# Seven block products in another order, with each bank read by one engine per product

## The chip, the cores and the metric

The kernel runs on one core of one Trainium2 chip. The time is device microseconds of one execution; three executions of the kernel before give a median of 2688.93 us (2687.47 to 2691.13). Five engines work side by side, each with its own queue of instructions: TensorE (PE, with its weight loads as PEld), VectorE (DVE), ScalarE (ACT), GpSimd (POOL) and SyncE (SP). TensorE writes its products to PSUM, which this kernel divides into eight banks of 128 x 512 fp32 each; VectorE and ScalarE read them from there into SBUF.

## The reference: what is computed

The input x has 16 samples of 256 channels and 32 x 32 places. Each sample goes through four layers, all in fp32:

- L0: group norm, q, k and v by 1x1 convolutions, softmax(q·k / 16) over the 1024 places, the weighted sum of v, an output projection, and x added.
- L1: mean and maximum over the channels, two 3x3 convolutions with one output channel, a sigmoid, and the sample multiplied by it.
- L2: like L0 with its own weights.
- L3: q and k of 32 channels, clipped logits, a softmax, the weighted sum of v times gamma, and x added.

```python
xn = group_norm(x, gamma, beta)
attn = jax.nn.softmax(jnp.einsum('bnc,bcm->bnm', q, k) / math.sqrt(C), axis=-1)
out = jnp.einsum('bnm,bmc->bnc', attn, v)                        # L0, L2
energy = jnp.clip(jnp.einsum('bqn,bqm->bnm', q, k) * scale, -10.0, 10.0)
out = jnp.einsum('bcm,bnm->bcn', v, jax.nn.softmax(energy, -1))  # L3
```

## The kernel before

**Two lanes.** Samples 0, 2, 4, ... run in lane 0 and 1, 3, 5, ... in lane 1. Each lane is a Python generator, `stream(0)` and `stream(1)`; they are stepped in turn, the second 30 steps behind the first, so that one sample's matmuls fill the other's waits. A scheduler then sets the final order of each engine's instructions and puts in the semaphores. The last sample's L3 has code of its own, `ending()`, which the change leaves alone.

**Attention.** The weights of L0 and L2 are folded first, so `attend` (L952) needs one product t = m·x in place of q and k, then the values v, then for each half of the queries `logits` (t·x into e, exponentials in place) and `weighted` (e·v). In L3 q and k are computed directly (L1109), the scores s at L1135, their exponentials at L1151 and the clipping at L1160; the values and `weighted` are the same.

**Seven products for eight.** Each of these large products is split into 2 x 2 blocks and computed with seven block products by a scheme of Strassen and Winograd: factors s1 to s4 and t1 to t4 are sums of blocks of the left and right factor, made by VectorE (for the weighted sum at L722, L723, L768 and L773), and partial products are summed in PSUM. Of the four result blocks, (0,0) is 11·11 + 12·21; the others are sums in which the running bank b holds first 11·11, then adds s2·t2, then adds s3·t3, and the bank c holds s1·t1 and then adds s4·22. In the code a product is written `go(left, right, bank)` and ends in `product` (L570), whose matmul is L577, the line that all of them show in the profile. With `fresh=False` it adds to what the bank holds.

**`seven` (L615)** is this scheme for the transform t (banks `tb`, `ta`, `tc`, `tf`), the values (`vb`, `va`, `vc`, `vf`) and the logits (`sb`, `sa`, `sc`, `sf`). `copy(i, j, ps)` is ScalarE's first write of result block (i, j), at L969 for t, L947 for v, L696 for the logits; `plus(i, j, ps)` is VectorE's addition of a bank to a block in SBUF, at L627. In the logits each pair of block rows is followed by its exponentials on ScalarE (L706, L708) as soon as the row is whole.

**`weighted` (L711)** writes the scheme out with three banks: b and c as above, and one bank `af` of which the halves hold 12·21 (`af[:, 0]`) and 22·(-t4) (`af[:, 1]`). Its result is acc in SBUF, of 128 x 4 x 256. Copies by ScalarE stand at L765, L778, L781 and L790, VectorE's additions at L749. v has a column of ones behind its 256, so the bank c gets the sums of the exponentials as a 129th column; their reciprocals are taken from c at L777 and L784, and `done` (L754) multiplies acc by them and adds it to the residual.

**Banks.** Every product takes its bank from one pool of eight, `ps_m`, by `bank()`. A bank is taken again in turn, once its last reader is through. Two engines that touch the same bank are put in order by a semaphore, also where both only read it.

Of the kernel before, what the change touches and what calls it, by code (L numbers as in the profile page):

```python
# [10 lines left out]
FP = mybir.dt.float32  # L11
# [5 lines left out]
P = 128  # L17
C = 256
# [5 lines left out]
TPH = HALF // P  # L24
# [4 lines left out]
STRIP = 32  # L29
# [178 lines left out]
def fast_path(nc, tc, k, bad, x, w_l0, w_l2, w_l3, qk_bias, v_bias, tap_idx, out):  # L208
# [7 lines left out]
    with ExitStack() as ctx:  # L216
# [5 lines left out]
        combp = ctx.enter_context(tc.tile_pool(name="combp", bufs=2))  # L222
# [10 lines left out]
        def bank(nm):  # L233
            return ps_m.tile([P, HALF], FP, tag="m", name=nm)
# [335 lines left out]
        def product(terms, fresh=True, lone=True):  # L570

            first = None
            for i, (out, pairs) in enumerate(terms):
                for m, (left, right) in enumerate(pairs):
                    mm = nc.tensor.matmul(  # L577
                        out,
                        left,
                        right,  # L580
                        start=fresh and m == 0 and (lone or i == 0),
                        stop=(m == len(pairs) - 1),
                        skip_group_check=True,
                    )
                    if first is None:
                        first = mm
                    elif m == 0 and not lone:
                        tc.add_manual_dep(
                            mm.ins,
                            first.ins.name,  # L590
                            mybir.DependencyInfo(
                                mybir.DependencyClass.NoSync, mybir.DependencyReason.DATA
                            ),
                            reason="the first product clears the bank's flags",
                        )
# [19 lines left out]
        def seven(go, copy, block, banks, left, right):  # L615

            b, a, c, f = banks

            def plus(i, j, ps):
                dst = block(i, j)
                if len(dst.shape) == 4:
                    src = ps.rearrange("p (a b n) -> p a b n", a=dst.shape[1], b=dst.shape[2])
                else:
                    src = ps.rearrange("p (m n) -> p m n", m=dst.shape[1])
                nc.vector.tensor_tensor(dst, src, dst, ALU.add)  # L627

            go(left("11"), right("11"), b, lone=False)
            copy(0, 0, b)  # L630
            go(left("12"), right("21"), a)
            plus(0, 0, a)
            yield
            go(left("s1"), right("t1"), c, lone=False)
            copy(1, 1, c)
            go(left("22"), right("-t4"), f)
            yield
            go(left("s2"), right("t2"), b, fresh=False)
            copy(0, 1, b)
            go(left("s4"), right("22"), c, fresh=False)  # L640
            plus(0, 1, c)
            yield
            go(left("s3"), right("t3"), b, fresh=False)
            copy(1, 0, b)
            plus(1, 1, b)
            plus(1, 0, f)
            yield

        def factors(blocks, sums):
# [61 lines left out]
        def weighted(e, vt, tv, y, ri, h, nm):  # L711


            hp = HALF // 2

            def a(i, kk):

                return e[:, kk * TPH : (kk + 1) * TPH, i * hp : (i + 1) * hp]

            s1 = combp.tile([P, TPH, hp], FP, tag="cb", name=f"cb_{nm}_{h}")  # L720
            s2, s3, s4 = a(0, 0), a(1, 0), a(0, 1)
            nc.vector.tensor_tensor(s1, a(1, 0), a(1, 1), ALU.add)  # L722
            nc.vector.tensor_tensor(s3, a(0, 0), s3, ALU.subtract)  # L723

            def vb(kk, j, n=P):
                return vt[:, kk * NT + j : (kk + 1) * NT : CC, :n]

            def go(left, right, out, fresh=True, lone=True):
                product(
                    [  # L730
                        (
                            out[:, i, : right.shape[-1]],
                            [(left[:, m, i * P : (i + 1) * P], right[:, m, :]) for m in range(TPH)],
                        )
                        for i in range(2)
                    ],
                    fresh,
                    lone,
                )

            t1, t2, t3, t4 = tv
            n0, n1 = h * TPH, h * TPH + 2

            c1, c2 = slice(0, P), slice(P, C)
            lo, hi = slice(0, 2), slice(2, 4)
            acc = combp.tile([P, TPH, C], FP, tag="acc", name=f"acc_{nm}_{h}")

            def plus(ts, cs, ps):
                nc.vector.tensor_tensor(acc[:, ts, cs], ps, acc[:, ts, cs], ALU.add)  # L749

            def done(i):
                t = h * TPH + i
                to = y[:, :, t, :]
                nc.vector.scalar_tensor_tensor(  # L754
                    to,
                    acc[:, i, :].rearrange("p (s j) -> p s j", j=STRIP),
                    ri[:, t : t + 1],
                    y[:, :, t, :],
                    ALU.mult,
                    ALU.add,  # L760
                )

            b = bank(f"b_{nm}_{h}")[:, : 2 * P].rearrange("p (i c) -> p i c", i=2)
            go(a(0, 0), vb(0, 0), b, lone=False)
            nc.scalar.copy(acc[:, lo, c1], b)  # L765
            yield
            af = bank(f"af_{nm}_{h}").rearrange("p (w i c) -> p w i c", w=2, i=2)
            nc.vector.tensor_tensor(s2, s1, s2, ALU.subtract)  # L768
            go(a(1, 1), t4, af[:, 1])
            yield  # L770
            go(a(0, 1), vb(1, 0), af[:, 0])
            plus(lo, c1, af[:, 0])
            nc.vector.tensor_tensor(s4, s4, s2, ALU.subtract)  # L773
            yield
            c = bank(f"c_{nm}_{h}")[:, : 2 * (P + 1)].rearrange("p (i c) -> p i c", i=2)
            go(s1, t1, c, lone=False)
            nc.vector.reciprocal(ri[:, n1 : n1 + 2], c[:, :, P])  # L777
            nc.scalar.copy(acc[:, hi, c2], c[:, :, :P])  # L778
            yield
            go(s2, t2, b, fresh=False)  # L780
            nc.scalar.copy(acc[:, lo, c2], b)  # L781
            yield
            go(s4, vb(1, 1, P + 1), c, fresh=False)
            nc.vector.reciprocal(ri[:, n0 : n0 + 2], c[:, :, P])  # L784
            plus(lo, c2, c[:, :, :P])
            for i in range(2):
                done(i)
            yield
            go(s3, t3, b, fresh=False)
            nc.scalar.copy(acc[:, hi, c1], b)  # L790
            plus(hi, c2, b)
            plus(hi, c1, af[:, 1])
            for i in range(2, 4):
                done(i)
            yield
# [156 lines left out]
        def attend(xt, y, weights, lane, nm, then):  # L952
# [22 lines left out]

            banks = [bank(f"t{q}_{nm}") for q in "bacf"]
            yield from seven(t_go, t_copy, t_block, banks, left, right_of(m, mc))


# [5 lines left out]
            for h in range(NH):  # L985
                e = expp.tile([P, NT, HALF], FP, tag="e", name=f"e_{nm}_{h}")
                yield from logits(left, tt, e, h, nm)
                do_chores(lane)
                yield from wait(W_AV)
                yield from weighted(e, vt, tv, y, ri, h, nm)  # L990

                then(h, tt.rearrange("p h c n -> p h (c n)"))
# [103 lines left out]
        def clipped_attend(xt, y, lane, b):  # L1096
# [336 lines left out]
            for h in range(NH):  # L1433
                e = exps(h)
                for mh in range(NH):
                    ss = score_products(h, mh)
                    for i in range(2):
                        exponentials(ss, e, mh, i)
                        clip(e, mh, i)
                    yield from wait(W_EXP)  # L1440
                yield from wait(W_AV3)
                yield from weighted(e, vt, tv, y, ri, h, f"l3_{b}")
                if b == B - 2 and h:
                    late.append((y, b))
                    yield
                    continue
                turn_strips(y, half(h))
                chores[lane].extend(in_pairs(y, half(h), bstrip3))
                chores[lane].append(functools.partial(store_tokens, y, b, h))
                yield  # L1450
# [384 lines left out]
```

## Time and profile before

| what | value |
|---|---|
| median of 3 runs | 2688.93 us (2687.47 to 2691.13) |
| profiled execution | 2688.37 us |
| its span in the profile | 2686.6 us |
| mean granted TensorE clock | 0.998 of full |
| TensorE, matmuls | 2653.6 us busy (99%), 18998 |
| VectorE | 2144.1 us busy (80%), 4180 |
| ScalarE | 1332.6 us busy (50%), 2825 |
| L696, copy of a logits product, 128 x 512 | 584 ns, 384 from b |
| L627, addition to a logits block, 128 x 512 | 686 ns |
| L778, copy of c, 128 x 256 | 368 ns, 94 times |
| L749, addition in `weighted`, 128 x 256 | 403 to 416 ns |
| L777, reciprocal of c's sums, 128 x 2 | 158 ns |

How to read it: the span runs from the first to the last instruction that the profiler shows; the execution's own time is 1.8 us longer. A busy matmul may contain waiting, since the ends of matmuls are modelled. In lists of groups, a row gives line, engine, operation, output and inputs by their names in the program, the count, busy time and mean, then the engine's idle time ahead of them and what released it. In a row of waits, `A <- B: 11.9, 45, 0.6` says that A was idle for 11.9 us in 45 places, at most 0.6 us each, until B was done.

### The profile page before, as it was taken

To read this page: it belongs to the slowest core of one execution; us is meant where nothing else is said; L and a number is where in the kernel's file an instruction comes from. 1 tells how busy PE (TensorE), PEld (TensorE's weight loads), DVE (VectorE), ACT (ScalarE), POOL (GpSimd) and SP (SyncE) were. 2 spreads that over 40 slices of the span, in tenths; PEclk is the share of its full clock that TensorE was granted. 3 is DMA by queue.
4 is the path that set the end of the run, shared out by engine and by line. 5 is a ranking of instruction groups with operands and counts; after the bars stand their busy time and mean duration, and the time that the engine had idled before them with its cause. 6 is when DMAs were issued, how large, how long until landed. Compare 5 with 4: busy or idle time off the path is not lost.

```text
span 2686.6 us, 47733 instructions
## 1 busy us (share of the span) xinstructions
PE 2653.6 (99%) x18998; PEld 2362.2 (88%) x18998; DVE 2144.1 (80%) x4180; ACT 1332.6 (50%) x2825; POOL 68.1 (3%) x172
## 2 busy tenths in 40 slices
PE   8999999999999999999999999999999999999998
PEld 7888898888988889889889898998989889898898
DVE  7888877888778887788867888678886788877777
ACT  4454445444455445544455545555454544545443
POOL 4100000000000000000000000000000000000000
PEclk9999999999999999999999999999999999999999
DMA  4021211112021120211201212112111121101111
GB/s 116 1 63 48 63 25 36 57 43 77 11 51 52 40 71 9 56 48 48 64 17 48 63 32 64 32 33 64 48 48 32 32 64 48 48 17 32 48 40 41
DMA packets 135877, 123.07 MB, mean 46 GB/s; under 512 B 12768, under 2 KB 126688, under 8 KB 135648
## 3 DMA queue, kind: packets, MB, share of 16 engines
q1 hardware_dynamic: 133776, 118.76, 16.1%
q8 instruction: 152, 2.49, 0.4%
q10 hardware_dynamic: 1872, 1.18, 0.1%
q14 instruction: 77, 0.63, 0.1%
HBM read 69.58 MB, written 50.33 MB: 45 GB/s over the span
## 4 chain that ended last, share of the span: by engine, by line
PE 79%; DVE 14%; ACT 3%; issue 2%; DMA 1%; POOL 0%; DVEq 0%; SPq 0%; ACTq 0%; POOLq 0%
PE b_l L577 15%; PE af_l L577 11%; PE c_l L577 11%; PE sb_l L577 10%; PE sc_l L577 8%; PE sf_l L577 4%; PE sa_l L577 4%; PE vb_l L577 3%; PE tb_l L577 2%; PE s L1135 2%; PE vc_l L577 2%; PE tc_l L577 2%; DVE e_l L627 1%; DVE vt L627 1%; PE qk L1109 1%
## 5 line engine op out<-in xcount | busy, mean ns | idle before, releaser
L696 ACT COPY e_l<-sb_l 128x512 f32<-128x512 f32 x384 | 222.2, 584 | 215.7 <-PE sb_l L577 214.5
L577 PE MATMUL sb_l<-t_l,x 128*128 128x256 f32 x1024 | 261.9, 386 | 0.5 <-ACT e_l L696 0.2
L577 PE MATMUL b_l<-vt,e_l 128*128 128x128 f32 x2048 | 251.8, 275 | 0.0
L577 PEld LDWEIGHTS b_l<-vt,e_l 128*128 128x128 f32 x2048 | 244.2, 192 | 5.4 <-issue 2.3
L577 PEld LDWEIGHTS sb_l<-t_l,x 128*128 128x128 f32 x1024 | 180.0, 190 | 40.6 <-ACT e_l L696 11.9
L706 ACT ACTIVATE e_l<-e_l 128x512 f32<-128x512 f32 x256 | 160.7, 629 | 87.6 <-DVE e_l L627 86.4
L708 ACT ACTIVATE e_l<-e_l 128x1024 f32<-128x1024 f32 x128 | 135.4, 1058 | 118.8 <-DVE e_l L627 118.7
L577 PE MATMUL c_l<-tv,cb_l 128*128 128x129 f32 x1504 | 185.0, 275 | 0.0
L627 DVE TENSOR_TENSOR e_l<-sc_l,e_l 128x512 f32<-128x512 f32 x128 | 87.8, 686 | 118.9 <-PE sc_l L577 117.3
L577 PEld LDWEIGHTS c_l<-tv,cb_l 128*128 128x128 f32 x1504 | 176.6, 191 | 6.5 <-PE qk L1109 3.1
L493 ACT ACTIVATE xr<-xr,bstrip 128x128 f32<-128x128 f32 (+1 forms) x376 | 134.1, 441 | 43.8 <-DVE xr L500 43.8
L947 ACT COPY vt<-vb_l 128x512 f32<-128x512 f32 x141 | 82.8, 587 | 142.8 <-PE vb_l L577 141.7
L1151 ACT ACTIVATE e<-s 128x512 f32<-128x512 f32 x256 | 132.0, 605 | 28.3 <-PE s L1135 27.6
L778 ACT COPY acc_l<-c_l 128x256 f32<-128x256 f32 x94 | 34.6, 368 | 205.1 <-DVE ri_l L777 155.3
L577 PE MATMUL af_l<-tv,e_l 128*128 128x128 f32 x1024 | 131.5, 278 | 4.3 <-ACT e_l L706 4.3
L577 PE MATMUL sc_l<-tc_l,xs_l 128*128 128x256 f32 x512 | 133.5, 383 | 2.3 <-DVE vt L627 2.3
L577 PE MATMUL sc_l<-t_l,xs_l 128*128 128x256 f32 x512 | 133.0, 382 | 0.8
L577 PE MATMUL sa_l<-t_l,x 128*128 128x256 f32 x512 | 132.3, 381 | 0.0
L577 PE MATMUL sb_l<-tc_l,xs_l 128*128 128x256 f32 x512 | 131.5, 379 | 0.0
L577 PE MATMUL sf_l<-tc_l,x 128*128 128x256 f32 x512 | 131.4, 379 | 0.0
L1160 DVE TENSOR_SCALAR e<-e 128x1024 f32<-128x1024 f32 x128 | 82.9, 684 | 60.0 <-ACT e L1151 60.0
L577 PEld LDWEIGHTS af_l<-tv,e_l 128*128 128x128 f32 x1024 | 121.2, 192 | 10.8 <-ACT e_l L706 7.7
(304 smaller groups left out, 5994.1 us busy)
## 6 DMA issues: line engine op xcount, KB each, us to landing
x<-mid_x SPq DMA_DIRECT2D x64, 512.0 KB, 3.3
xr<-in_x_dram SPq DMA_DIRECT2D x64, 256.0 KB, 5.1
mid_x<-t_z SPq DMA_DIRECT2D x128, 128.0 KB, 2.3
mid_x<-t_l SPq DMA_DIRECT2D x128, 128.0 KB, 2.3
x<-in_x_dram SPq DMA_DIRECT2D x62, 256.0 KB, 4.0
out_dram<-xr SPq DMA_DIRECT2D x124, 128.0 KB, 2.3
raw_l<-in_w_l_dram SPq DMA_DIRECT2D x1, 1024.0 KB, 6.7
raw_l<-in_w_l_dram SPq DMA_DIRECT2D x2, 256.0 KB, 5.4
```

Of the source, the lines that this page charges most:

```text
L493: nc.scalar.activation(y[:, s, ts], y[:, s, ts], AF.Identity, bias=bias[:, s : s + 1])
L577: mm = nc.tensor.matmul(out, left, right, start=fresh and m == 0 and (lone or i == 0), stop=(m == len(pairs) - 1), skip_group_check=True,)
L627: nc.vector.tensor_tensor(dst, src, dst, ALU.add)
L696: nc.scalar.copy(block(i, j), ps.rearrange("p (m n) -> p m n", m=2))
L706: nc.scalar.activation(part, part, AF.Exp)
L708: nc.scalar.activation(e[:, m : m + 2, :], e[:, m : m + 2, :], AF.Exp)
L778: nc.scalar.copy(acc[:, hi, c2], c[:, :, :P])
L947: nc.scalar.copy(block(i, j), ps.rearrange("p (m n) -> p m n", m=TPH))
L1109: nc.tensor.matmul(ps[i * PH : (i + 1) * PH, : qt * P].rearrange("p (g n) -> p g n", g=qt), w3qk[:, c, i], xt[:, g0 : g0 + qt, c], start=( ...
L1135: nc.tensor.matmul(ss[g][:, j * 2 * P : (j + 1) * 2 * P].rearrange("p (t g j) -> p t g j", t=TPH, g=2), qk[gs, mh, 1 - blk, j * P : (j + 1 ...
L1151: nc.scalar.activation(by_strip[:, :, :, qa], ss[g].rearrange("p (m t n) -> p m t n", m=2, t=TPH), AF.Exp,)
L1160: nc.vector.tensor_scalar(part, part, EXP_MIN, EXP_MAX, ALU.max, ALU.min)
```

## The change

In `seven`, the product s2·t2 and its copy go ahead of 22·(-t4). The product 22·(-t4), in bank f, is now copied by ScalarE as the first part of block (1,0). After the last product, s3·t3, VectorE adds bank b to both blocks (1,1) and (1,0); before, ScalarE copied b to (1,0), and VectorE added b to (1,1) and f to (1,0).

In `weighted`, 22·(-t4), the second half of `af`, is copied by ScalarE to acc after VectorE's addition from the first half; after the last product VectorE makes two additions from b, and ScalarE's copy of b there (L790) is gone. acc gets one column more, and ScalarE copies c whole, with the column of sums. The reciprocal of the second half's sums is taken from acc and not from c, and stands just ahead of the last product.

```diff
@@ seven
             copy(1, 1, c)
-            go(left("22"), right("-t4"), f)
-            yield
             go(left("s2"), right("t2"), b, fresh=False)
             copy(0, 1, b)
+            yield
+            go(left("22"), right("-t4"), f)
+            copy(1, 0, f)
             go(left("s4"), right("22"), c, fresh=False)
             plus(0, 1, c)
             yield
             go(left("s3"), right("t3"), b, fresh=False)
-            copy(1, 0, b)
             plus(1, 1, b)
-            plus(1, 0, f)
+            plus(1, 0, b)
             yield
@@ weighted
-            acc = combp.tile([P, TPH, C], FP, tag="acc", name=f"acc_{nm}_{h}")
+            acc = combp.tile([P, TPH, C + 1], FP, tag="acc", name=f"acc_{nm}_{h}")
...
-                    acc[:, i, :].rearrange("p (s j) -> p s j", j=STRIP),
+                    acc[:, i, :C].rearrange("p (s j) -> p s j", j=STRIP),
...
             plus(lo, c1, af[:, 0])
+            nc.scalar.copy(acc[:, hi, c1], af[:, 1])
             nc.vector.tensor_tensor(s4, s4, s2, ALU.subtract)
...
             go(s1, t1, c, lone=False)
-            nc.vector.reciprocal(ri[:, n1 : n1 + 2], c[:, :, P])
-            nc.scalar.copy(acc[:, hi, c2], c[:, :, :P])
+            nc.scalar.copy(acc[:, hi, P:], c)
...
             yield
+            nc.vector.reciprocal(ri[:, n1 : n1 + 2], acc[:, hi, C])
             go(s3, t3, b, fresh=False)
-            nc.scalar.copy(acc[:, hi, c1], b)
             plus(hi, c2, b)
-            plus(hi, c1, af[:, 1])
+            plus(hi, c1, b)
```

## The prediction

> **What bounds the kernel now.** I read the page first: busy shares, then the chain that ended last.
>
> ```profile
> PE 2653.6 (99%) x18998; PEld 2362.2 (88%) x18998; DVE 2144.1 (80%) x4180; ACT 1332.6 (50%) x2825; POOL 68.1 (3%) x172
> PE 79%; DVE 14%; ACT 3%; issue 2%; DMA 1%; POOL 0%; DVEq 0%; SPq 0%; ACTq 0%; POOLq 0%
> ```
>
> TensorE sets the time; VectorE is the second engine, at 80%. But 99% busy hides small holes, because a matmul that waits is drawn as a longer one. So I took the start times of all matmuls and compared neighbours: an undisturbed distance is 111 ns (128 columns), 112 (129), 216 (256) or 430 (512). What stands beyond that sums to 81.2 us: 10.8 in the first 67 us, 5.9 after 2620 us and 64 in the steady part. The windows view confirms that this steady part is TensorE's, at full clock:
>
> ```profile
> 67.00:2620.00 2553.00, 2537.85 (x18151) 2260.25 (x18150) 2043.44 (x3956) 1275.47 (x2701) 40.24 (x102) 1.00 0.16 44
> ```
>
> The change can win no more than its share of these 81.2 us. Sorted by product, the largest entries are: the `weighted` product a(1,1)·t4, 11.1 us in 62 places; `seven`'s last product s3·t3, 11.0 in 107; the first product of the transform t, 6.9 in 31; `weighted`'s s4 product into c, 6.3 in 39; the logits' s1 product, 5.6 in 26; the logits' s4 product, 3.6 in 28. The clipped scores, the gate and qk hold 17 together, which the change does not touch. The waits view names who is waited for (idle us, times, longest):
>
> ```profile
> ACT acc_l L778 <- DVE ri_l L777: 155.3, 55, 6.1
> DVE e_l L627 <- ACT e_l L696: 46.9, 43, 1.6
> PEld sb_l L577 <- ACT e_l L696: 11.9, 45, 0.6
> PEld af_l L577 <- ACT e_l L706: 7.7, 22, 0.4
> PEld c_l L577 <- ACT acc_l L778: 6.6, 15, 0.7
> PEld tb_l L577 <- PE sa_l L577: 6.5, 8, 0.8
> PEld sc_l L577 <- DVE vt L627: 5.1, 7, 0.7
> ```
>
> Loads run ahead, so these rows show where, and only roughly how much. Two chains can be seen whole in the timeline (start, us, engine; brackets: idle before, releaser). In `weighted`:
>
> ```profile
> 1804.91 0.37 DVE L749 TENSOR_TENSOR acc_l<-af_l,acc_l 128x256 f32<-128x256 f32 x1
> ...
> 1806.53 0.13 DVE L777 RECIPROCAL ri_l<-c_l 128x2 f32<-128x2 f32 x1
> ...
> 1806.69 0.37 ACT L778 COPY acc_l<-c_l 128x256 f32<-128x256 f32 x1 [6.05 <-DVE ri_l L777]
> ...
> 1807.12 2.05 PE L577 MATMUL c_l<-vt,e_l 128*128 128x129 f32 x16 [0.26 <-ACT acc_l L778]
> ```
>
> ScalarE was free for 6 us and c's product was done; it waited for a reciprocal that stood in VectorE's queue behind sums and the next norm. In `seven`, bank b:
>
> ```profile
> 1854.03 0.59 ACT L696 COPY e_l<-sb_l 128x512 f32<-128x512 f32 x1 [1.14 <-PE sb_l L577]
> ...
> 1854.67 1.59 PEld L577 LDWEIGHTS sb_l<-t_l,x 128*128 128x128 f32 x8 [0.21 <-ACT e_l L696]
> ```
>
> One product (4 matmuls, 860 ns) lies between b's second and third use. The copy needs 200 ns from matmul end to start, 584 to run and 52 to release: about 840 ns. Any small delay of ScalarE becomes a hole.
>
> **What the Trainium skill says.** "PSUM — Partial Sum Buffer", section "PSUM bank collisions raise a hardware error": two engines must not touch a bank at once, two reads included, so a dependency is put between them. The trace agrees: L778 and L777 both only read c, and L778 waited 204.3 us on it in 63 of 94 places. The section "Engine vs sequencer instructions" there: ScalarE's and VectorE's queues are strict first-in-first-out, while TensorE may load weights early but starts its matmuls in order. It agrees: 6 us of ScalarE's idle time ahead of one copy above, and loads that begin 0.1 to 0.2 us before their matmuls.
>
> **The change, part by part.** No engine gets more work: per `seven` 4 copies and 4 additions remain, per `weighted` 4 and 4. The copy of c grows from 2x128 to 2x129 elements (368 ns, up by about 1 ns), the new af copy replaces the old last copy (368 each). TensorE's instructions are the same, but in the built programs its matmuls with a semaphore wait of their own rise from 401 to 625. In the trace of before such matmuls start a median of 0 to 1 ns late, so 224 more cost nothing to 0.1 us if they are already fulfilled; the upper bound, 94 ns each (their 90th percentile), is 21 us, and I take 0.5.
>
> *a. Cover of b in `seven`.* Counting matmuls between b's uses in the two orders: second to third use had one product (860 ns) in 48 of 128 logits and 9 of 32 transforms; after, 1 of 128, the rest at least 1720 ns against 840 needed. The first-to-second cover shrinks where the scheduler had put other work between: 8 logits fall to 860 ns, 8 transforms stand at 1720. Of the 11.0 us I take 9.5 away and put 1 back.
>
> *b. Two additions from b at the end of `seven`.* Before, VectorE waited for ScalarE's copy: it started 818 ns after s3's end in 71 of 128 logits (32 of 47 values, 7 of 32 transforms), now 200, so both additions end 0.6 us earlier there. The row's exponentials move with them, and those are what a(1,1)·t4 waits for (7.7 us in the waits). Its 62 holes average 0.18 us, well below 0.6; but exponentials also queue on ScalarE. I take 7.5 of the 11.1. VectorE's wait of 46.9 us goes too; that is idle time, worth something only where VectorE is late.
>
> *c. c's copy without reciprocal.* It started a mean of 1876 ns after c's product, could at 200; its holes, 6.3 us, go where only the copy is late: near 1807 the other thing waited for, s4 from L773, ended at 1806.48, before TensorE was free, so that hole's 0.26 us go. Where L773 itself is late they stay; I take 4 of 6.3. The reciprocal now reads SBUF and stands behind the first half's results, before L790's additions; nothing but L754 of the second half needs it.
>
> *d. Bank rotation.* Eight handovers of values to logits lose 0.59 us each, because the logits' c takes a bank last read by VectorE's addition:
>
> ```profile
> 2001.46 1.13 PE L577 MATMUL sc_l<-tc_l,xs_l 128*128 128x256 f32 x4 [0.32 <-DVE vt L627]
> ```
>
> In the changed program that matmul waits for an exponential at L1151 instead, which is over by then (1999.84 plus 1.63). I take 4 of 4.7.
>
> *e. What it adds.* At the 8 places where a logits stage meets the next L2 transform, the order puts s2·t2 ahead of the transform and the norm (L147) behind both last additions:
>
> ```profile
> 1856.46 0.69 DVE L627 TENSOR_TENSOR e_l<-sb_l,e_l 128x512 f32<-128x512 f32 x1
> 1857.07 0.80 DVE L147 TENSOR_SCALAR x<-x,a_l,bb_l 128x1024 f32<-128x1024 f32 x1
> 1857.97 1.10 PE L577 MATMUL tb_l<-x,m_l 128*128 128x512 f32 x2 [0.44 <-PE sa_l L577]
> ```
>
> L147 now waits for one or two more additions of about 0.6 us, while TensorE fills 0.86 of that with the moved product: the hole, 0.68 now, becomes about 1.05, and the next product loses 0.3. I take 0.75 x 8 = 6 us (bounds 0 and 1.3 x 8 = 10). At the 8 even handovers L924/L925, combining the transform's inputs, stand behind two additions of 411 ns: 0.25 x 8 = 2 (bounds 0 and 0.8 x 8 = 6). In `weighted` the af copy waits on ScalarE for L749's addition of af; that one ends before c's product in 88% of places, up to 3.15 us after in the rest, and c's copy is queued behind it: within the 2.3 left in c.
>
> Sum: −9.5 −7.5 −4 −4 = −25; +1 +6 +2 +0.5 = +9.5; together −15.5. Slices of 8 us show VectorE at 95 to 100% in several stretches (1811 to 1835 for one): there an earlier release only shifts the hole to the next VectorE-bound product. I give back a quarter of what b and c save and a little, 3.5. That leaves −12 us on the profiled 2688.37 (its span is 2686.6, the other 1.8 stay): 2676.4. The median of the runs is 0.6 above the profile: **2677**.
>
> **Rivals.** *Holes only move* (within 5.4 us): if VectorE's lateness re-emerges for two thirds of the 25, 8 us are gained, e and the small terms take 9.5 back: 2690. For it: 80% busy, full stretches. Against it: VectorE gets 46.9 us of waiting back, and the largest holes are behind ScalarE. *Nearly all goes*: e costs nothing since TensorE's moved products cover it; −25 gives 2664. *Slower, by the handover*: the norm's delay at L147 in the 8 odd places and the like in the 8 even ones. If the pair of additions, each a bank wait behind TensorE's last product, holds the norm for 2.5 us and not 0.75, 16 x 2.5 = 40 us and the small terms of 5 stand against the 25: 20 slower, 2709. It makes the change slower by over 0.2% from about 1.6 us per handover (25.4 over 16). For it: at these places VectorE's queue is the only way to the next transform, as 1857 shows. Against: the order moves L147 by additions whose inputs are ready 1.3 us later at most. *It does not do what it says* can be left out: the built order has two products between b's uses nearly everywhere, and no wait of L778 on L777.
>
> **How the numbers follow.** Chances: forecast (−5.4 to −19) 0.58; nearly all, 0.08; holes move, 0.16; slower 0.18. Faster by over 0.2% (5.4 us, about what a measurement of this kernel can tell from no change) is the first two, 0.66. The forecast's own range is 2670 to 2683. The range for 8 in 10 takes the third case and the mild half of the last: 2663 to 2696.
>
> **What would show it.** Right: in the waits, L778 no longer behind L777, and the wait of `e_l L627` on L696 near zero; s3·t3's holes below 2 us, a(1,1)·t4's below 4; `sc_l` behind `vt L627` gone; the odd handovers' `tb_l` holes near 1 us. Wrong: if holes in the transform's first products or in qk grow by more than 15 us, or if matmuls with fulfilled waits start 50 ns or more late, which would add 11 us or more across the kernel.

## The result, and the profile after

The changed kernel takes 2681.31 us (median of 9 runs, 2678.34 to 2683.05), the kernel before 2689.45 (9 runs). The ratio is 0.9969, with a 95% interval of 0.9959 to 0.9979: 8.1 us or 0.3% faster, in the predicted direction and range, and two thirds of the 12 us forecast.

The profiled execution took 2683.05 us, the highest of the nine, with a span of 2681.3. Its page, busy time and the chain that ended last:

```profile
PE 2646.6 (99%) x18998; PEld 2361.7 (88%) x18998; DVE 2149.9 (80%) x4180; ACT 1332.2 (50%) x2825; POOL 68.5 (3%) x172
PE 89%; DVE 7%; ACT 1%; issue 1%; DMA 1%; POOL 0%; SPq 0%; DVEq 0%; ACTq 0%
```

No engine has other work than before, but the chain has: VectorE's share fell from 14% to 7% and ScalarE's from 3% to 1%. The page alone would promise much. The windows view of the steady part corrects that (us, then busy time of PE, PEld, DVE, ACT and POOL, the granted clock as a share of full, the DMA engines' busy share and GB/s):

```profile
67.00:2620.00 2553.00, 2537.45 (x18224) 2266.00 (x18224) 2057.12 (x3972) 1276.40 (x2703) 40.52 (x103) 1.00 0.16 44
```

In the same stretch of time TensorE did 18224 matmuls and not 18151, at the same busy time. The gain is 73 matmuls more in the same time, and no busy share shows it.

Where the waits went (idle us, times, longest):

```profile
ACT acc_l L773 <- DVE acc_l L749: 231.7, 71, 5.7
ACT acc_l L778 <- PE c_l L577: 67.7, 48, 4.5
DVE e_l L627 <- ACT e_l L696: 29.6, 15, 3.8
PEld tb_l L577 <- ACT t_l L969: 16.8, 16, 1.2
PEld af_l L577 <- ACT e_l L706: 4.9, 14, 0.8
PEld sb_l L577 <- ACT e_l L696: 4.0, 18, 0.3
```

L778 waits for its product now, not for the reciprocal; the wait of 204 us has a successor of 232 in the new copy L773, and in the trace no engine waits for that copy. VectorE's wait for ScalarE's copies at L627 fell from 46.9 to 29.6 us and not to nearly nothing: by the list of groups the addition from the logits' b lost its 45.5, but the addition from c now waits 26.3 for the copy of b. The logits' bank b has lost two thirds of its loads' waits (11.9 to 4.0). What has grown is `tb`, the transform.

As in the prediction I compared neighbouring starts of matmuls with their undisturbed distance, and sorted the excess by product. The table holds the steady part, from 67 to 2600 us; "odd" and "even" are the transforms of L2 of odd and even samples. All later tables are made in this way, and differences in the text are taken before rounding.

| holes on TensorE, us | before | after |
|---|---|---|
| logits, s3·t3 | 7.1 | 0.8 |
| weighted, a(1,1)·t4 | 11.1 | 7.5 |
| weighted, s4 into c | 6.2 | 1.1 |
| logits, s1·t1 into c | 5.0 | 0.8 |
| the gate | 4.4 | 1.9 |
| transform, odd samples | 5.4 | 10.4 |
| transform, even samples | 1.5 | 9.3 |
| all | 64.2 | 57.5 |

The first five rows give 21.6 us; the transforms take 12.7 of it back, and smaller places 2.2. The sum is 6.7 us less. The two profiled spans differ by 5.3 and not by 8.1, since the execution profiled after is the slowest of its nine; outside the steady part, the holes grew by some 1.8 us, so that those of the whole trace fall by about 4.9. In the same way, over whole traces, the holes of each of the 12 kernels below differ from those of the kernel before by as much as the spans do, to within 1.7 us. The start and the end of the program hold 12 to 16 us of holes that vary from run to run, which the tables leave out.

The even handover, where the seven products of one lane's transform follow the other lane's `weighted`, in the timeline after:

```profile
1806.34 0.75 DVE L749 TENSOR_TENSOR acc_l<-b_l,acc_l 128x256 f32<-128x256 f32 x2
...
1807.08 0.68 DVE L925 TENSOR_TENSOR xs_l<-xs_l,x 128x512 f32<-128x512 f32 x1
1807.68 0.87 DVE L754 SCALAR_TENSOR_TENSOR xr<-acc_l,ri_l,xr 128x256 f32<-128x256 f32 x2
...
1807.91 1.10 PE L577 MATMUL tb_l<-xs_l,mc_l 128*128 128x512 f32 x2 [0.38 <-DVE xs_l L925]
...
1808.26 0.42 ACT L1043 ACTIVATE junk<-xr 128x256 f32<-128x256 f32 x1 [0.65 <-DVE xr L754]
...
1808.48 0.68 DVE L926 TENSOR_TENSOR xs_l<-x,xs_l 128x512 f32<-128x512 f32 x1
...
1809.07 0.67 ACT L969 ACTIVATE t_l<-tc_l,tb_l 128x512 f32<-128x512 f32 x1
1809.08 1.21 DVE L1035 TENSOR_REDUCE pl<-xr 128x4 f32<-128x1024 f32 x1
...
1809.79 1.13 PE L577 MATMUL tc_l<-xs_l,m_l 128*128 128x512 f32 x2
1810.21 0.68 DVE L927 TENSOR_TENSOR x<-x 128x512 f32<-128x512 f32 x1
...
1811.03 0.67 PE L577 MATMUL tb_l<-x,m_l 128*128 128x512 f32 x1
```

Three products start late, with what follows them: s2 by 0.61 us, s4 by 0.19 and s3 by 0.36. s2 begins just after VectorE has made its factor (L925), s3 just after L927. s4 has its factor at 1809.16 and starts at 1809.79: it waits for bank c, whose copy (L969) stood in ScalarE's queue behind two of the other lane's means over the channels (L1043), and these waited for VectorE's results (L754). Ahead of the factors and the copy stand the other lane's additions (L749), results, means and maximum (L1035). They are ready earlier than before, because the change releases them earlier, and the scheduler's order now has them first. That it goes by what is ready first is read from these orders; the runs e5 to e8 and e12 test the order, not the scheduler's reason. In the kernel before, the factor and the copy come first:

```profile
1811.90 0.69 DVE L925 TENSOR_TENSOR xs_l<-xs_l,x 128x512 f32<-128x512 f32 x1
...
1812.50 0.42 DVE L749 TENSOR_TENSOR acc_l<-b_l,acc_l 128x256 f32<-128x256 f32 x1
1812.83 0.42 DVE L749 TENSOR_TENSOR acc_l<-af_l,acc_l 128x256 f32<-128x256 f32 x1
1813.16 0.68 DVE L926 TENSOR_TENSOR xs_l<-x,xs_l 128x512 f32<-128x512 f32 x1
...
1813.57 0.69 ACT L969 ACTIVATE t_l<-tc_l,tb_l 128x512 f32<-128x512 f32 x1 [0.22 <-PE tc_l L577]
...
1814.23 1.02 PE L577 MATMUL tb_l<-xs_l,mc_l 128*128 128x512 f32 x2
```

There s2 had its factor 1.6 us ahead of time, and bank c was copied as soon as its product was done.

### The profile page after: what moved, and what is told of

It is laid out like the page before. It is cut to its first block, busy times and chain, and to the rows that moved or that the text cites. A ratio compares the mean times of both kernels' runs of the same rounds, so it can differ in the third digit from the quotient of the medians.

```text
span 2681.3 us, 47925 instructions
## 1 busy us (share of the span) xinstructions
PE 2646.6 (99%) x18998; PEld 2361.7 (88%) x18998; DVE 2149.9 (80%) x4180; ACT 1332.2 (50%) x2825; POOL 68.5 (3%) x172
## 4 chain that ended last, share of the span: by engine, by line
PE 89%; DVE 7%; ACT 1%; issue 1%; DMA 1%; POOL 0%; SPq 0%; DVEq 0%; ACTq 0%
PE b_l L577 16%; PE sb_l L577 12%; PE af_l L577 11%; PE c_l L577 11%; PE sc_l L577 8%; PE vb_l L577 5%; PE sf_l L577 4%; PE sa_l L577 4%; PE vc_l L577 3%; PE tb_l L577 3%; PE s L1135 2%; PE tc_l L577 2%; PE vf_l L577 2%; PE va_l L577 2%; PE qk L1109 1%
## 5 line engine op out<-in xcount | busy, mean ns | idle before, releaser
L577 PE MATMUL sb_l<-t_l,x 128*128 128x256 f32 x1024 | 255.9, 381 | 0.0
L696 ACT COPY e_l<-sb_l 128x512 f32<-128x512 f32 x256 | 150.1, 586 | 141.9 <-PE sb_l L577 141.1
L577 PEld LDWEIGHTS sb_l<-t_l,x 128*128 128x128 f32 x1024 | 185.4, 191 | 32.2 <-issue 10.3
L627 DVE TENSOR_TENSOR e_l<-sc_l,e_l 128x512 f32<-128x512 f32 x128 | 88.0, 687 | 125.4 <-PE sc_l L577 98.7
L627 DVE TENSOR_TENSOR e_l<-sb_l,e_l 128x512 f32<-128x512 f32 x256 | 165.7, 680 | 4.8 <-ACT e_l L696 0.5
L773 ACT COPY acc_l<-af_l 128x256 f32<-128x256 f32 x94 | 34.8, 371 | 231.7 <-DVE acc_l L749 231.7
L577 PE MATMUL b_l<-tv,e_l 128*128 128x128 f32 x1024 | 128.0, 275 | 0.0
```

The costliest lines, as they stand in the source:

```text
L577: mm = nc.tensor.matmul(out, left, right, start=fresh and m == 0 and (lone or i == 0), stop=(m == len(pairs) - 1), skip_group_check=True,)
L696: nc.scalar.copy(block(i, j), ps.rearrange("p (m n) -> p m n", m=2))
L773: nc.scalar.copy(acc[:, hi, c1], af[:, 1])
```

## The experiments: the parts of the change

Theory: the change removes bank waits as foreseen, and the loss comes from the queues, VectorE's above all, whose order the scheduler changes when work becomes ready earlier. Rivals: the order of the products itself is at fault in the transform; the removed waits were cover anyway; the gain needs both parts together. All times below are medians with the interval of the ratio to the kernel before.

**e1: `seven` alone.**

The kernel has `seven` as in the changed kernel and `weighted` as in the kernel before.

> Only seven's part of the change, weighted as before. If the entries of the two hole tables simply belong to the two parts, this has: last product of seven -7.0, the logits' first c product -4.7, a(1,1)*t4 -3.6, the gate's c -2.5, the transform after odd handovers +5, after even handovers some +4: about -9 us against before (2680), nearly the whole measured gain. Rival: the two parts need each other, because VectorE's queue is full until weighted lets it go; then not more than -4 (2685).

2678.81 us, ratio 0.9961 (0.9947 to 0.9974): 10.5 us less than the kernel before. The intervals of this and of the whole change overlap, so that no difference between the half and the whole is shown. And that with the wait of L778 on the reciprocal still there:

```profile
ACT acc_l L778 <- DVE ri_l L777: 162.5, 42, 6.1
ACT acc_l L778 <- DVE ri L777: 49.0, 8, 6.1
```

**e2: `weighted` alone.**

The kernel has `seven` as in the kernel before and `weighted` as in the changed kernel.

> Only weighted's part, seven as before. Same theory: its second c product -5.1, its first +0.8; at the even handovers VectorE now has the two additions ahead of L925 and the maximum L1035 ahead of L927, so the transform's last product waits, +3 to +6; sum -3 to +2 us (2686 to 2691). Rival: the handover's loss belongs to seven alone; then -4 to -5 (2685).

2684.20 us, 0.9983 (0.9976 to 0.9989), 5.2 us less than the kernel before and a larger gain than expected. The c product gave 3.8 us, and the even handover took 7.8, more than the 3 to 6 expected; not foreseen were gains of 3.9 in front of a(1,1)·t4 and 2.8 at the gate. The rival, that the handover's loss belongs to `seven` alone, falls: the loss is whole here. It does not belong to `weighted` alone either: e1 lost 6.3 at the even handovers, in other products, 5.5 of it in front of the transform's first and 2.2 in front of s2. Either half is enough, and the losses do not add.

**e9, e10: the two halves of `seven`.** e9 has the new order of products with the readers of before:

```diff
-            go(left("22"), right("-t4"), f)
-            yield
             go(left("s2"), right("t2"), b, fresh=False)
             copy(0, 1, b)
+            yield
+            go(left("22"), right("-t4"), f)
```

> The kernel before with only the order of the products changed in seven: s2*t2 and its copy ahead of 22*(-t4); the readers stay (ScalarE copies b to block (1,0), VectorE adds f). Theory: the cover of bank b alone removes the holes in front of the logits' last product (7.1 to 0.8), at the price of 1.5 in front of s2*t2; VectorE's order at the handovers is the one of before, so the odd handovers keep 0.68 us, a(1,1)*t4 keeps its 11 and the logits' c its 5: 4 to 6 us less than before (2684). Rival: the holes belong to ScalarE's three copies per seven in a row, and stay without the other readers: 2688 to 2690.

e10 has the readers, with the order of before:

```diff
             go(left("22"), right("-t4"), f)
+            copy(1, 0, f)
             yield
...
-            copy(1, 0, b)
             plus(1, 1, b)
-            plus(1, 0, f)
+            plus(1, 0, b)
```

> The kernel before with only the readers changed in seven: 22*(-t4) is copied by ScalarE, and VectorE adds b twice after the last product; order as before. Theory: exponentials come 0.6 us earlier, a(1,1)*t4 falls from 11.1 to about 2 as with seven alone, the logits' c product loses its wait (5.0 to 0.8), but the last products keep most of their 7.1 us, and both handovers' losses are here (odd +4, even +5): 2684 to 2687. Rival: the readers have none of the gain, then 2690 or more, since the handovers' losses stay.

e9: 2685.27 us, 0.9985 (0.9979 to 0.9992). e10: 2685.68, 0.9987 (0.9980 to 0.9993). Both theories held in the main; in e9 the holes of s3·t3 fell to 2.7 and not to 0.8.

| holes, us | before | e9 order | e10 readers | e1 both | e2 weighted | e11 copy of c | after |
|---|---|---|---|---|---|---|---|
| logits, s3·t3 | 7.1 | 2.7 | 6.6 | 0.8 | 7.8 | 6.7 | 0.8 |
| a(1,1)·t4 | 11.1 | 12.2 | 1.6 | 1.6 | 7.2 | 10.3 | 7.5 |
| s4 into c | 6.2 | 5.8 | 3.4 | 2.3 | 2.4 | 1.6 | 1.1 |
| logits, s1·t1 | 5.0 | 5.3 | 0.8 | 0.8 | 5.4 | 5.4 | 0.8 |
| gate | 4.4 | 4.6 | 4.5 | 5.1 | 1.6 | 3.0 | 1.9 |
| transform, odd | 5.4 | 5.4 | 10.2 | 9.6 | 5.9 | 5.4 | 10.4 |
| transform, even | 1.5 | 1.2 | 7.6 | 7.8 | 9.3 | 8.2 | 9.3 |
| all | 64.2 | 59.8 | 63.4 | 55.9 | 61.9 | 62.6 | 57.5 |

The order alone frees the bank b and costs nothing at the handovers, although s2 is asked for one product earlier: with VectorE's old order its factor is in time. The rest of s3·t3 goes with the readers. The readers alone free the exponentials and the logits' c, and bring the whole loss at the odd handovers and 6.1 us at the even ones. In e10, with the order of before, 12.8 us of loads' waits on the logits' bank b stay:

```profile
PEld sb_l L577 <- ACT e_l L696: 12.8, 56, 0.5
```

**e11: the copy of c alone.**

```diff
-            nc.vector.reciprocal(ri[:, n1 : n1 + 2], c[:, :, P])
-            nc.scalar.copy(acc[:, hi, c2], c[:, :, :P])
+            nc.scalar.copy(acc[:, hi, P:], c)
...
+            nc.vector.reciprocal(ri[:, n1 : n1 + 2], acc[:, hi, C])
             go(s3, t3, b, fresh=False)
```

Here acc has its additional column too, in lines not shown.

> The kernel before with one part of weighted changed: ScalarE copies c whole without waiting for the reciprocal, which reads SBUF later; the last product's readers stay. Theory: this alone takes the 5 us in front of the second c product away; of the even handovers' loss only what VectorE's new order brings (both additions now stand ahead of L925, the results ahead of L926), 2 to 5 us: 2685 to 2688. Rival: the waits of 204 us of L778 were almost all cover, and nothing is won: 2689 to 2692.

2687.03 us, 0.9993 (0.9984 to 1.0001): too near to no change to be told from it. Its holes say why. ScalarE's longest wait for VectorE, L778 behind L777, is gone, s4 into c gains 4.6 us, and the even handover takes 6.8.

## The experiments: VectorE's queue

**e3: the old order in the transform alone.**

```diff
-            yield from seven(t_go, t_copy, t_block, banks, left, right_of(m, mc))
+            yield from seven(t_go, t_copy, t_block, banks, left, right_of(m, mc), early=False)
```

Here `early=False` puts 22·(-t4) and its copy ahead of s2·t2, as in the kernel before.

> The changed kernel, but in the transform t alone 22*(-t4) stays ahead of s2*t2 (the readers stay changed). In the changed kernel the even handovers lose 0.61 us in front of s2*t2, 0.19 before s4 and 0.36 before s3. Theory: VectorE's queue sets the end there (L925 behind two additions, L927 behind the maximum L1035), so the hole in front of s2 goes but reappears in front of s3, about 1 us each: the time equals the changed kernel's within 1.5 us. Rival: the order of the products is the cause, s2 being asked for one product too early; then 8 holes of 0.6 go and 4 to 5 us are won (2677).

2679.75 us, 0.9966 (0.9954 to 0.9978), 1.6 below the changed kernel and inside its interval. The trace decides more sharply: the even transforms lose 9.31 us, and lost 9.26. The hole in front of s2 went (4.9 to 0) and came back in front of s4 (1.5 to 6.5), not of s3 as I had expected:

```profile
1805.35 0.42 ACT L1054 ACTIVATE junk<-xr 128x256 f32<-128x256 f32 x1 [0.65 <-DVE xr L765]
...
1805.77 0.40 ACT L1054 ACTIVATE junk<-xr 128x256 f32<-128x256 f32 x1
...
1806.16 0.67 ACT L980 ACTIVATE t_l<-tc_l,tb_l 128x512 f32<-128x512 f32 x1
...
1806.88 1.12 PE L577 MATMUL tc_l<-xs_l,m_l 128*128 128x512 f32 x2 [0.54 <-ACT t_l L980]
```

L1054, L765 and L980 are L1043, L754 and L969 of the changed kernel. The factor of s4 was there at 1806.26; bank c was copied late, behind the means. The order of the products is not the cause of the loss; that it is two queues and not one was new.

**e4: and the maximum later.**

```diff
+            yield from wait(5)
+            maximum(1)
-            yield from wait(W_PLANES)
+            yield from wait(W_PLANES - 5)
```

`maximum(1)` is L1035 of the second half, taken out of `planes`, the function that had it.

> As the run before, and the maximum over the channels of the second half (L1035, 1.21 us on VectorE) is emitted five steps later, so that VectorE forms s3 (L927) ahead of it at the even handovers. Theory: now s2 has its product of cover and s3 its operand in time, the holes there fall from 1.16 to about 0.2 us, 7 to 8 us less than the changed kernel (2674). Rival: the gate, which needs the maximum, pays it back; then no gain beyond 2 us.

2680.56 us, 0.9964 (0.9952 to 0.9977): nothing. The hole in front of s4 stayed (6.45 us), that in front of s3 fell by only 0.5, and the gate lost 1.2. The expectation failed in its place: s4 waits for a copy that does not depend on the maximum. Nor does s3 come in time. Its factor (L938, which is L927) now stands ahead of the maximum and is ready 1.2 us before s3 starts, but the copy that frees bank `tb` (L980) is not: it stands on ScalarE behind the late copies of c and f.

```profile
1809.01 0.69 DVE L938 TENSOR_TENSOR x<-x 128x512 f32<-128x512 f32 x1
...
1810.14 0.68 ACT L980 ACTIVATE t_l<-tb_l,tb_l 128x512 f32<-128x512 f32 x1
...
1810.88 0.70 PE L577 MATMUL tb_l<-x,m_l 128*128 128x512 f32 x1
```

So two queues set this place, and to relieve one leaves the other.

The next four runs add edges to VectorE's queue, without a semaphore. An edge says which of two instructions comes first on the engine; `behind_of(late, early)` makes one. `HAND1`, `HAND2` and `HAND3` are constants that switch the edges of e5, e6 and e7 on; the lines that note the instructions in `marks` are not shown.

**e5: statistics behind the logits' last additions.**

```diff
+                    if HAND1 and step == 3 and h and g and nm[:2] == "l0" and b_of(nm) % 2:
+                        for late in marks["stats"]:
+                            behind_of(late, marks["sums"][-1])
```

> The changed kernel with one edge added in VectorE's queue, without a semaphore: in the odd samples' L0, second half, the statistics of the other lane's L2 norm (L114) come behind the last two additions of the logits. In the changed kernel the scheduler puts two of them (0.68 us each) ahead, and a(1,1)*t4 then loses 0.47 us in 8 places, 4.5 in all; in the run with seven alone they stand behind, and the loss is not there. Theory: these 4.5 us go (and the norm of the odd samples also comes to stand one addition earlier, which may give up to 4 more): 2673 to 2677. Rival: the norm of the even samples is then late, as the 5.5 us in front of the transform's first product in the run with seven alone suggest; then no gain (2681).

In the changed kernel the statistics of the other lane's norm (L114) come first, and a(1,1)·t4 waits in its middle for the last exponential:

```profile
1791.83 1.28 DVE L114 BATCH_NORM_STATS2 st_l<-x 128x6 f32<-128x512 f32 x2
...
1793.02 1.27 DVE L627 TENSOR_TENSOR e_l<-sb_l,e_l 128x512 f32<-128x512 f32 x2
1793.60 0.61 PE L577 MATMUL af_l<-tv,e_l 128*128 128x128 f32 x4
1793.73 0.63 ACT L706 ACTIVATE e_l<-e_l 128x512 f32<-128x512 f32 x1 [1.15 <-DVE e_l L627]
...
1794.41 0.38 PE L577 MATMUL af_l<-tv,e_l 128*128 128x128 f32 x1 [0.20 <-ACT e_l L706]
```

With the edge, the additions (L648 in this kernel) come first, and the product runs through:

```profile
1788.98 1.29 DVE L648 TENSOR_TENSOR e_l<-sb_l,e_l 128x512 f32<-128x512 f32 x2
...
1790.19 1.28 DVE L117 BATCH_NORM_STATS2 st_l<-x 128x6 f32<-128x512 f32 x2
1790.57 1.95 PE L582 MATMUL af_l<-tv,e_l 128*128 128x128 f32 x16
```

2675.05 us, 0.9941 (0.9927 to 0.9954): 6.3 less than the changed kernel, and the intervals do not meet. a(1,1)·t4 falls to 3.1, the odd transforms to 4.5 (the edge let their norm come earlier as well); s4 into c pays 4.8 back, and the gate 1.5.

**e6: the norm ahead of an addition.**

```diff
+                    if HAND2 and step == 0 and h and g and nm[:2] == "l2" and b_of(nm) % 2 == 0:
+                        behind_of(marks["sums"][-1], marks["norm"])
```

> The changed kernel with one other edge in VectorE's queue: at the odd handovers the addition of the logits' second product (L627, 0.69 us) comes behind the norm's scaling (L147), as it did in the kernel before; nothing else of VectorE's work moves by more than a few places. Theory: the hole in front of the transform's first product falls from 1.30 to about 0.6 us, 8 x 0.7 = 5 to 6 us less (2676). Rival: TensorE waits there for the scaling on ScalarE (L150) or for the norm's constants, and nothing is won (2681).

The odd handover after the change, where the addition from `sa` stands ahead of the norm (L144, L147):

```profile
1851.24 1.12 PE L577 MATMUL sb_l<-tc_l,xs_l 128*128 128x256 f32 x4
...
1851.72 0.69 DVE L627 TENSOR_TENSOR e_l<-sa_l,e_l 128x512 f32<-128x512 f32 x1
1852.32 0.15 DVE L144 TENSOR_TENSOR bb_l<-vec,bb_l 128x2 f32<-128x2 f32 x1
1852.51 0.81 DVE L147 TENSOR_SCALAR x<-x,a_l,bb_l 128x1024 f32<-128x1024 f32 x1
...
1853.42 0.67 PE L577 MATMUL tb_l<-x,m_l 128*128 128x512 f32 x1 [1.06 <-issue]
```

With L147 (L150 in this kernel) ahead of the last of them:

```profile
1847.22 1.12 PE L582 MATMUL sb_l<-tc_l,xs_l 128*128 128x256 f32 x4
1848.01 0.81 DVE L150 TENSOR_SCALAR x<-x,a_l,bb_l 128x1024 f32<-128x1024 f32 x1
...
1848.92 1.10 PE L582 MATMUL tb_l<-x,m_l 128*128 128x512 f32 x2 [0.58 <-PE sb_l L582]
```

From the last logits product to `tb` it is 1.70 us here and 2.18 in the changed kernel. The median is 2677.83, 0.9953 (0.9940 to 0.9967), 3.5 less, but the interval overlaps that of the changed kernel, so that the time alone does not show it; the holes of the odd transforms fall by 3.9. The mechanism is right, the size was 5 to 6: the norm's constants (L134 to L144) are still made between the additions from `sb`.

**e7: factors ahead of results, and e8: all edges.** e7 is e3 with these edges; e8 has those of e5, e6 and e7.

```diff
+            if early:
+                for late in marks["done"]:
+                    behind_of(late, s4)
+                for late in marks["max"]:
+                    behind_of(late, s3)
```

> The kernel with the transform's old order of products, and at the even handovers VectorE forms s4 and s3 (L926, L927) ahead of the two final results of the other lane's weighted (L754) and of the maximum (L1035). With the old order alone 0.81 us stood in front of s4 and 0.36 in front of s3, and moving the maximum alone left them. Theory: VectorE's two results ahead of L926 are what is left of the cause; the holes fall to 0.2, about 7 us less than the old order alone (2673). Rival: the later results and maximum make the gate late and are paid back there (2679).

> The edges of the three runs before, with the transform's old order of products. If the three losses stand in different places, their gains add: 4.5 + 5.5 + 7 = 17 less than the changed kernel, 2664. If they are one queue's lateness that only moves on, not more than the best of the three alone, about 2673.

e7: 2679.86 us, 0.9965 (0.9952 to 0.9979), the same as e3. With the results (L754) later, the means are later too, and bank c's copy passes them: s4's hole fell from 6.5 to 0.7 us. But s3 lost 2.0 more, and s4 into c 1.2; 2.7 us fewer holes did not show in the median (the two profiled spans differ by 2.0). e8: 2672.68, 0.9941 (0.9927 to 0.9955). The gains do not add to 17: it is 8.6 less than the changed kernel by the medians, 7.5 by the ratios, with 6.8 us fewer holes, and its ratio is e5's. The rest stands in other places: s3 of the even transforms (4.9), s4 into c (6.4), the gate (3.5). The first of them is not VectorE's:

```profile
1803.44 0.42 ACT L1090 ACTIVATE junk<-xr 128x256 f32<-128x256 f32 x1 [0.34 <-DVE xr L791]
...
1804.26 0.67 ACT L1015 ACTIVATE t_l<-tb_l,tb_l 128x512 f32<-128x512 f32 x1
...
1804.98 1.12 PE L582 MATMUL tb_l<-x,m_l 128*128 128x512 f32 x2 [0.34 <-ACT t_l L1015]
```

The copy that frees `tb` (L1015) stands in ScalarE's queue behind two means (L1090) that wait for VectorE's results, which e7 had put back.

**e12: and the copy ahead of the means.** This is e8 with one edge in ScalarE's queue; L1094 is L1090 of e8.

```diff
+                if (i, j) == (0, 1) and nm[:2] == "l2" and lane == 0:
+                    for late in marks["means"]:
+                        behind_of(late, copied_t)
```

> The kernel with all three edges and the old order in the transform, and one edge in ScalarE's queue: at the even handovers the second copy of the transform's bank b (L1015) comes ahead of the last two means over the channels (L1090), which wait for VectorE's late results. In the run with all edges, s3*t3 of the transform loses 0.61 us in 8 places, 4.9 us in all, behind that copy. Theory: this hole is ScalarE's first-in-first-out queue alone and goes, as VectorE has s3 in time: 4 to 5 us less than with all edges, 2668. Rival: the means make the gate late, or VectorE's queue sets the end there after all; 2672 as with all edges.

2670.61 us, 0.9935 (0.9922 to 0.9949), the fastest kernel of this study. The copy comes at once, and the hole goes from 4.9 to 0.7 us:

```profile
1801.50 0.69 ACT L1015 ACTIVATE t_l<-tb_l,tb_l 128x512 f32<-128x512 f32 x1 [0.17 <-PE tb_l L582]
1802.09 0.40 ACT L1094 ACTIVATE junk<-xr 128x256 f32<-128x256 f32 x1
...
1802.25 1.11 PE L582 MATMUL tb_l<-x,m_l 128*128 128x512 f32 x2
```

The gate, which the means feed, pays 2.6 of it back (3.5 to 6.0). Both expectations were half right. By the ratios it is 1.6 us below e8; the two intervals overlap, so that of the two steps only that from the changed kernel to e12 is shown by the time.

## Why the prediction came out as it did

The forecast, 2677, was right in sign and range and 4 us too low. By its own steps, with the holes of the two traces:

- *a, cover of b:* right in mechanism; e9 shows 4.4 us by the order alone. Of 11.0 us it took 9.5 and gave 1 back. The logits gave 6.3, with 1.5 lost in front of s2; the values gave nothing (1.4 before and after, steady part), and the transform's share is counted below. The term was too large by some 3.5.
- *b, two additions and earlier exponentials:* the mechanism is right (e10: 9.5 us), the size 3.6 and not 7.5. What takes it back is named by e5: in 8 places the scheduler puts L114 ahead of the two additions, 4.5 us. I had reckoned with the 0.6 us that each addition starts earlier, and not with other work being put in front of it.
- *c, copy of c:* 5.1 against 4, but not all of it is the copy's: in e1 the same hole shrinks by 3.9 with the copy still behind the reciprocal. And e11 shows that the step was priced without its consequence: the same release brings the loss at the even handovers.
- *d, bank rotation:* 4.1 against 4. It comes from the readers (e10), not from the order (e9).
- *e, odd handovers:* 5.0 against 6, right; e6 shows that it is the norm behind the additions.
- *e, even handovers:* this is the step that failed most in size: 7.8 us against 2. The difference, 5.8, is more than what the forecast missed. I priced one factor (L925) behind two additions. The trace shows three late products in a row, two behind VectorE's factors and one behind a copy on ScalarE, which I had not looked at; e3 shows that the sum counts and not the first hole, e7 and e12 that the copies behind the means are part of it.
- *waits on TensorE:* priced at 0.5. TensorE's queue shows 407 separate wait instructions before and 630 after. Where the distance is known (389 and 573 places), the next matmul starts a median of 1 ns late in both traces, with a 75th percentile of 1 and 2 ns: most of the added waits cost nothing that shows. The latest tenth starts 3 ns late or more before and 74 ns or more after; whether the wait costs that or what it waits for was not separated.
- *a quarter given back:* 3.5 for VectorE's full stretches. It was a rough stand-in for what a and b lost against their forecast, 7.6 together.

The gate, which I had called untouched, gained 2.5 us; the gain comes with `weighted` (2.8 in e2). That the sum came so near is in part luck: a, b and the even handovers were too favourable by some 13 us together, and c, the odd handovers, the waits, the quarter and the gate too unfavourable by some 9.

Of the signs of being right, two came: L778 no longer waits for L777, and `sc_l` no longer for `vt L627`. Three did not: a(1,1)·t4 stayed at 7.5, L627's wait at 29.6, and the odd handovers' hole grew to 1.3 us. The holes of s3·t3 are below 2 us in the logits alone (0.8); the values' 1.4 and the even transforms' 2.9 stand beside them. No sign of being wrong came, but the transforms' 12.7 us more are not far from the 15 that it named.

*Holes only move* was the rival nearest to what happened: of 21.6 us gained in the five rows above, 12.7 came back at the handovers, or 59%; it had assumed that two thirds of 25 come back, and the terms of e besides. *Slower, by the handover* had the right place: 12.7 us over 16 places are 0.8 each, half of the 1.6 from which it would have decided.

Two sections of the Trainium skill's "PSUM — Partial Sum Buffer" carry parts of this. "PSUM bank collisions raise a hardware error" has a dependency put between two engines that touch one bank, two readers included. This bears on c, and the traces agree: with the second reader of c gone, its wait of 204.3 us is gone, and L778 waits for its product (67.7 us). "Engine vs sequencer instructions" calls the queues of ScalarE and VectorE strict first-in-first-out, and the traces agree: in the even handover above the transform's first product in bank c ended at 1807.53, and its copy, behind the means, began at 1809.07; in e12 one edge in that queue took the hole at s3 from 4.9 us to 0.7.

What stays open: why `seven` and `weighted` together give less than the sum of the two (8.1 against 10.5 and 5.2). The holes point to a(1,1)·t4, where e1 gained 9.5, e2 3.9 and both only 3.6, and e5 shows the statistics' place as its cause in the whole change; that the scheduler sets them there because of `weighted` was not tried by itself.

## What to carry to other kernels

- When a second engine is 80% busy and a scheduler orders its queue, a release that is moved forward can also move other work forward, into the queue ahead of something urgent. Compare that engine's order before and after, at each place where the bounding engine hands over, and price the whole chain of late operands and late copies there, not only the first.
- A long wait in a list need not be a dear one: 204 us of L778 were worth 4.6 us to TensorE, and nothing that the time could show.
- Bank cover and readers are two separate gains. The order of the products cost nothing at the handovers here; the earlier release did, and a few edges in two queues, with the transform's old order (e12), won about as much again as the change itself.

## What the runs showed that was not expected

Over 220 more wait instructions in TensorE's queue left its matmuls a median of 1 ns late, as before the change. And an edge in one queue is answered in another: the edges on VectorE in e7 cost 2.0 us behind a copy on ScalarE, and one edge there, against 4.2 us won, cost 2.6 at the gate (e12).
